# Value patches of a 5x5 correlation loaded in four transfers of 32 partitions, with the squares of pixels in another order

## The chip, the cores and the metric

The kernel runs on one core of a Trainium2 chip, as one launch. The metric is the device time of the launch in microseconds; three runs before the change gave 5152.57 (median), 5151.66 and 5160.39.

The core has five engines with a queue of instructions each: TensorE (PE: matmuls, and PEld, its weight loads), VectorE (DVE), ScalarE (ACT), GpSimd (POOL) and SyncE (SP). In this kernel SyncE issues every transfer; sixteen DMA engines carry them out. SBUF has 128 partitions; TensorE writes to PSUM, which DVE and ACT read.

## The reference

The input is x of shape (4, 512, 64, 64) in float32. Two layers follow each other. Layer 0 is linear attention with a second set of heads made by a depthwise 5x5 convolution:

```python
qkv = concat(h @ wq.T, h @ wk.T, h @ wv.T)          # 1536 channels
dw  = conv(qkv, dw_kernel 5x5, groups=1536)
pw  = conv(dw, pw_kernel 1x1, groups of 8)
f   = concat(qkv, pw) as heads of 24 channels: query 8, key 8, value 8
query, key = relu(...), relu(...)
scores = einsum("bhdn,bhen->bhde", [value, 1], key)   # sums over all 4096 pixels
out    = scores @ query, divided by its last row
y      = bn(proj_kernel @ out) + x
```

Layer 1 makes edge maps of y (Sobel, Laplace, diagonals), four 1x1 branches with GELU, a gate from their means, a 1x1 fusion, a norm over channels, GELU and a residual.

## The kernel before, in words

**Batches and groups.** There are four batches, each in four groups of 16 heads (128 channels per kind). A group works through keys, values and queries of its channels (`keys_and_values`, L544, and `queries`, L574, are lists of steps in a fixed order). The rest of layer 0 and all of layer 1 of a batch (`project_out`, `edge_branches`, `fuse_out`) are generators; `advance` (L868) calls them between the steps of the next batch's groups by planned costs, so that they fill TensorE. The order of TensorE's instructions is the one of the program; those of the other engines are put in order by a scheduler.

**Strips.** The 64x64 pixels of a batch go in eight strips of 512: each strip is every fourth row of one half of the image, eight rows of 64 pixels. `project` (L250) makes keys or queries of a strip and stores each in an SBUF tile `inp` in four transfers of 32 partitions (L266). `values` (L273) makes values with pixels on the partitions and writes them to a DRAM tensor `near` of blocks of four rows, 68 columns and 4 x 66 numbers per column (L291, four transfers a strip). Its borders are zeroed for the first two groups (L158: 34 rows, L160).

**The convolved heads.** Keys and queries are convolved directly on TensorE in 32x32 tiles (`convolve`, L382, 640 matmuls a half image). Values aren't: the scores of the convolved heads need the sum over pixels of convolved value times convolved key, so `correlate` (L432) multiplies convolved keys with the unconvolved values around each pixel, for all 5x5 shifts, and `weigh` (L454) takes the kernel's weights afterwards. The pixels are handled as squares of 4x4: in a contraction of 128, each partition stands for one square, 16 squares in a row of squares (x) by 8 rows of squares (b). A partition needs the values of its square and around it: 8 columns x 4 x 66 numbers of one block of rows in `near`, 8448 B in one run. That is a tile `near` of 128 x 2112 numbers, loaded by `load_near` (L420) in one transfer (L427), three buffers (`VALS`, L72), eight loads per group: two halves, two halves of the heads (jp), two blocks (b). Three are issued at the end of `keys_and_values`, then one each time two steps of `correlate` have used a tile up (L452).

**The order of squares.** The convolved keys come out of PSUM with the pixels in the order of the strip: row (8), x (16), n (4, the column in the square). ACT takes them out with ReLU, in the order column, x, row, and sums each partition's row by the way (`accum_out`, L402 to 405, `squares`, L109). Then `conv_turn` (L411) transposes 128 pixels at a time: one column n of all 128 squares, so that partition p holds square x = p // 8, row p % 8. The patch load uses the same order: its pattern in DRAM has 16 columns of squares, 8 rows of blocks and one run. `ksum` (L401) gathers the sums, two per bank (a half each), and `conv_sums` (L488) adds the halves.

What sets the order around the change: SyncE issues in its own order and stops at each transfer that has to wait. A patch load waits for the tile to be free (TensorE's last matmul on it) and for the stores into `near` (L291). The first matmul of `correlate` on a tile waits for its load.

Of the kernel before, what the change touches and what calls it, by code (L numbers as in the profile page):

```python
# [8 lines left out]
F32 = mybir.dt.float32  # L9
AF = mybir.ActivationFunctionType  # L10
ALU = mybir.AluOpType
AX = mybir.AxisListType

B, C, H, W = 4, 512, 64, 64
N = H * W
P = 128
# [11 lines left out]
BN1_SCALE = 1.0 / (1.0 + 1e-5) ** 0.5  # L28
SOBEL_EPS = 1e-8
LN_EPS = 1e-6  # L30

# [19 lines left out]
VROW = 4 * 66  # L53
# [21 lines left out]
def _span(d, n):  # L75

    return max(0, -d), n - max(0, d)
# [3 lines left out]
def conv_seq_kernel(  # L81
    ctx: ExitStack, tc, x, wqkv, dpk, wtab, proj, projc, pwk, bn0, consts, vec, watt1, batt1, watt2, wbr, wfuse, out
):
    nc = tc.nc
# [9 lines left out]
    mini = front.enter_context(tc.tile_pool(name="mini", bufs=2))  # L94
# [5 lines left out]
    def work_tile(name, n=512):  # L100
        return work.tile([P, 512], F32, tag="w", name=name)[:, :n]

    def ps_tile(name):
        return psum.tile([P, 512], F32, tag="ps", name=name)

    def quad_tiles(name):
        return [psum.tile([P, 512], F32, tag="quad", name=name) for _ in range(4)]

    def squares(ap):  # L109

        return ap.rearrange("p (b x n) -> p n x b", b=8, n=4)

    def rows(ap, width=W):
        return ap.rearrange("p (r c) -> p r c", c=width)
# [8 lines left out]
    def const_col(name, value):  # L123
        t = const.tile([P, 1], F32, name=name)
        nc.gpsimd.memset(t, value)
        return t
# [3 lines left out]
    grad_eps = const_col("grad_eps", 2 * SOBEL_EPS)  # L130
    ln_eps = const_col("ln_eps", LN_EPS)
    ones = const.tile([P, P], F32, name="ones")
# [82 lines left out]
    class Group:  # L215
# [166 lines left out]
        def convolve(self, t, half):  # L382
            banks = quad_tiles("cv")
            last = len(DXS) * 2 - 1
            for n, (dx, b) in enumerate((dx, b) for dx in DXS for b in range(2)):
                c0, c1 = _span(dx, W)
                for j in range(4):
                    for i in range(4):
                        q = slice(32 * i, 32 * i + 32)
                        nc.tensor.matmul(  # L390
                            rows(banks[i])[32 * j : 32 * j + 32, :, c0:c1],
                            lhsT=self.mat[t][q, j, (dx + 2) * 8 + 4 * b : (dx + 2) * 8 + 4 * b + 4, :],
                            rhs=inps[t][q, j, 8 * half + b : 8 * half + b + 8, c0 + dx : c1 + dx],
                            start=(n == 0), stop=(n == last),
                        )
            outs = []
            for i in range(4):
                o = work_tile("co")
                if t == KEY:
                    if half == 0 and i == 0:  # L400
                        self.ksum = mini.tile([P, 2, 4], F32, name="ksum")  # L401
                    nc.scalar.activation(  # L402
                        o.rearrange("p (n x b) -> p n x b", n=4, b=8), squares(banks[i]), AF.Relu,
                        accum_out=self.ksum[:, half, i : i + 1],
                    )
                else:
                    nc.scalar.activation(o, banks[i], AF.Relu)
                outs.append(o)
            self.conv[t] = outs
# [10 lines left out]
        def load_near(self, count):  # L420

            for _ in range(count):
                half, jp, b = at = next(self.nears, (None,) * 3)
                if half is not None:
                    self.near[at] = vals.tile([P, 8 * VROW], F32, name="near", tag="vals")
                    v = self.near_dram[jp, 8 * half + b]
                    nc.sync.dma_start(  # L427
                        out=self.near[at],
                        in_=bass.AP(v.tensor, v.offset, [[4 * VROW, 16], [(W + 4) * VROW, 8], [1, 8 * VROW]]),
                    )  # L430

        def correlate(self, half, jp, step):  # L432

# [54 lines left out]
        def conv_sums(self):  # L488

            total = mini.tile([P, 4], F32, name="ktotal")  # L490
            nc.vector.tensor_add(total, self.ksum[:, 0, :], self.ksum[:, 1, :])
            ps = ps_tile("ksum_ps")
            nc.tensor.matmul(ps[:, 0:4], lhsT=table["csum"], rhs=total, start=True, stop=True)
            self.kc = mini.tile([P, 4, 32], F32, name="kc_sb", bufs=1)
            for i in range(4):
                nc.vector.tensor_scalar(self.kc[:, i, :], hmask, ps[:, i : i + 1], None, ALU.mult)
# [531 lines left out]
```

## Time and profile before

| | |
|---|---|
| median of three runs | 5152.57 us |
| the profiled execution | 5156.95 us |
| its span (first to last instruction) | 5155.2 us |
| matmul clock granted, mean | 0.963 |
| HBM read, written | 622 MB, 214 MB |
| patch loads `near<-near` (L427) | 128 of 1056 KB, 138 MB; issue 556 ns median |
| matmuls of `correlate` (L442) | 8192, 330.7 us, 313 ns each |
| evictions of the convolved keys (L402) | 128 of 128x512, 597 ns each |

The page gives busy shares of each engine first, then the span in 40 slices, the DMA queue, the chain that ended last, and the costliest groups of instructions by line, operation and tiles. A name like `near<-near` is output and input; here the first is the tile in SBUF, the second the tensor in DRAM. Views of the trace list what each engine waited for and how long, the instructions in order of time, and the busy time, clock and DMA rate in a stretch that is asked for. The "DMA share" is the mean busy share of the sixteen DMA engines; it can pass 1 a little, where packets overlap.

### The profile page before, as it was taken

How to read it: one execution, taken by the hardware profiler on the slowest of the kernel's cores; microseconds unless marked ns; L12 is line 12 of the kernel's file. 1: busy time of each engine (PE TensorE's matmuls, PEld its weight loads, DVE VectorE, ACT ScalarE, POOL GpSimd, SP SyncE). 2: the span in 40 equal slices, each digit the busy share in tenths (PEclk: the TensorE clock that was granted, in tenths of full speed). 3: DMA queues.
4: the chain of work that ended last, by engine and by line, in shares of the span. 5: the costliest groups of instructions: out<-in, count | busy, mean ns of one | idle time of the engine just before them, and what ended most of it. 6: DMA issues, size and time to landing. Idle time of an engine off the chain costs nothing. (4 is left out here: it accounts for less than half of the span.)

```text
span 5155.2 us, 107053 instructions
## 1 busy us (share of the span) xinstructions
PE 4721.2 (92%) x46362; PEld 2727.4 (53%) x46362; DVE 2125.2 (41%) x2960; ACT 1622.7 (31%) x2585; POOL 384.0 (7%) x291
## 2 busy tenths in 40 slices
PE   7899999998999999799999998989989998899877
PEld 4556555454566655344466655444446565345443
DVE  1222221113655625211456543431135556246975
ACT  1111111001444524200235442430024445125765
POOL 0000000000000003200000000320000000000225
PEclk9999999999999999899999999999999999899989
DMA  6777777775666666767667666567666665674535
GB/s 184 187 193 195 185 212 191 179 160 140 194 184 193 194 191 188 212 153 150 168 178 208 170 191 186 180 202 172 154 177 173 178 183 160 176 179 117 153 103 169
DMA packets 645992, 910.30 MB, mean 177 GB/s; under 512 B 323688, under 2 KB 394376, under 8 KB 627088
## 3 DMA queue, kind: packets, MB, share of 16 engines
q1 hardware_dynamic: 645520, 903.45, 65.5%
q8 instruction: 364, 5.96, 0.5%
q14 instruction: 108, 0.88, 0.1%
HBM read 622.13 MB, written 213.98 MB: 162 GB/s over the span
## 5 line engine op out<-in xcount | busy, mean ns | idle before, releaser
L256 PE MATMUL proj<-xt,w_sb 128*128 128x512 f32 x2048 | 959.6, 611 | 58.3 <-DMA xt<-in_x 47.2
L642 PE MATMUL yps<-hd,fold_sb 128*128 128x512 f32 x2048 | 904.3, 598 | 25.2 <-DMA hd<-heads 23.1
L390 PE MATMUL cv<-inp,mat 32*32 32x512 f32 x20480 | 771.7, 621 | 121.2 <-issue 112.0
L256 PEld LDWEIGHTS proj<-xt,w_sb 128*128 128x128 f32 x2048 | 382.8, 195 | 534.8 <-issue 457.1
L642 PEld LDWEIGHTS yps<-hd,fold_sb 128*128 128x128 f32 x2048 | 385.8, 191 | 510.5 <-issue 474.2
L390 PEld LDWEIGHTS cv<-inp,mat 32*32 32x32 f32 x20480 | 422.1, 105 | 433.5 <-issue 270.8
L717 PE MATMUL br<-maps,wbr_sb 128*128 128x256 f32 x2048 | 491.6, 393 | 56.6 <-ACT maps L700 33.7
L278 PEld LDWEIGHTS val<-w_sb,xt 128*128 128x128 f32 x4096 | 471.5, 192 | 31.6 <-issue 21.9
L717 PEld LDWEIGHTS br<-maps,wbr_sb 128*128 128x128 f32 x2048 | 395.6, 196 | 173.5 <-issue 55.8
L278 PE MATMUL val<-w_sb,xt 128*128 128x128 f32 x4096 | 484.1, 276 | 0.1
L795 PE MATMUL zps<-ef,wf_sb 128*128 128x512 f32 x1024 | 462.6, 604 | 21.0 <-DVE z L799 7.2
L262 ACT COPY strip<-proj 128x512 f32<-128x512 f32 x256 | 149.3, 583 | 1017.1 <-PE proj L256 952.8
L647 DVE SCALAR_TENSOR_TENSOR yt<-yps,shift,xr 128x512 f32<-128x512 f32 x128 | 96.1, 751 | 905.1 <-PE yps L642 833.7
L442 PE MATMUL corr<-near,ckt 128*32 128x160 f32 x8192 | 330.7, 313 | 28.1 <-DMA near<-near 23.0
L236 POOL TENSOR_TENSOR mat<-dp_sb 128x1280 f32<-128x1280 f32 x32 | 77.3, 2416 | 3484.1 <-PE cv L390 2959.3
L795 PEld LDWEIGHTS zps<-ef,wf_sb 128*128 128x128 f32 x1024 | 194.2, 193 | 263.8 <-issue 227.8
L442 PEld LDWEIGHTS corr<-near,ckt 128*32 128x32 f32 x8192 | 252.4, 110 | 130.0 <-issue 58.2
L690 DVE TENSOR_TENSOR maps<-dv 128x1054 f32<-128x1054 f32 x128 | 162.6, 1270 | 304.1 <-PE br L717 304.1
L724 ACT ACTIVATE ef_o<-br,shift,scale 128x256 f32<-128x256 f32 x256 | 142.4, 560 | 314.9 <-PE br L717 314.4
L306 ACT ACTIVATE kt<-tr 128x512 f32<-128x512 f32 x128 | 76.1, 595 | 496.5 <-PE tr L304 488.9
L354 DVE RECIPROCAL rec<-rec 128x512 f32<-128x512 f32 x64 | 214.5, 3351 | 1.4
L402 ACT ACTIVATE co<-cv 128x512 f32<-128x512 f32 x128 | 74.6, 597 | 438.5 <-PE cv L390 438.4
(124 smaller groups left out, 4096.6 us busy)
## 6 DMA issues: line engine op xcount, KB each, us to landing
xt<-in_x SPq DMA_DIRECT2D x400, 512.0 KB
near<-near SPq DMA_DIRECT2D x128, 1056.0 KB
inp<-strip SPq DMA_DIRECT2D x1024, 64.0 KB
win<-y SPq DMA_DIRECT2D x128, 396.0 KB
near<-vt SPq DMA_DIRECT2D x512, 66.0 KB
y<-yt SPq DMA_DIRECT2D x128, 264.0 KB
yr<-y SPq DMA_DIRECT2D x128, 264.0 KB
xr<-in_x SPq DMA_DIRECT2D x128, 256.0 KB
```

Source lines behind the costliest of these rows:

```text
L256: nc.tensor.matmul(ps, lhsT=self.w[t][:, c, :], rhs=xs[self.b, j][c], start=(c == 0), stop=(c == NCH - 1))
L262: nc.scalar.copy(s, ps)
L278: nc.tensor.matmul(ps[:, ts(c, P)], lhsT=xs[self.b, j][n][:, ts(c, P)], rhs=self.w[VALUE][:, n, :], start=(n == 0), stop=(n == NCH - 1),)
L354: nc.vector.reciprocal(rec, rec)
L390: nc.tensor.matmul(rows(banks[i])[32 * j : 32 * j + 32, :, c0:c1], lhsT=self.mat[t][q, j, (dx + 2) * 8 + 4 * b : (dx + 2) * 8 + 4 * b + 4, :],
L442: nc.tensor.matmul(self.banks[jj][32 * i : 32 * i + 32, 160 * b : 160 * b + 160], lhsT=self.held["c", i][:, at : at + 32], rhs=v[:, 4 * n ...
L642: nc.tensor.matmul(ps, lhsT=fold_sb[g // NG][:, g % NG, ts(c, P)], rhs=hd[g], start=(g == 0), stop=(g == 2 * NG - 1),)
L647: nc.vector.scalar_tensor_tensor(yt[:, :, 1 : W + 1], rows(ps), shift0[:, c : c + 1], rows(xr), ALU.add, ALU.add)
L690: nc.vector.tensor_sub(flat[:, half : 3 * half - 2], dvs[:, 2 : 2 * half], dvs[:, 0 : 2 * half - 2])
L717: nc.tensor.matmul(rows(ps)[:, 4 * n : 4 * n + 4, :], lhsT=wbr_sb[:, k, c, :], rhs=rows(maps[c // 2][:, slot[k], c % 2, :], WB)[:, :, 0:W] ...
L724: nc.scalar.activation(o[:, n, :], ps[:, 256 * n : 256 * n + 256], AF.Gelu, bias=shift1[:, k : k + 1], scale=scale1[:, k : k + 1], accum_o ...
L795: nc.tensor.matmul(ps, lhsT=wf_sb[:, k, ts(c, P)], rhs=ef[k], start=(k == 0), stop=(k == 3))
```

## The change

A partition stands for another square. The 128 squares are cut in four quarters of 32: 8 columns of squares by 4 rows of squares. Partition p of the new order is quarter a, x half, then x (8), then row (4). So the patch load becomes four transfers, each to 32 partitions, with 8 columns of squares, 4 rows of blocks and the same run of 8448 B. The convolved keys have to come in the same order: each bank of 512 is taken out by two instructions of 256 pixels (four rows of the strip each) instead of one, with a sum each, so `ksum` has four sums per bank and `conv_sums` reduces them. Nothing else differs.

```diff
     def squares(ap):
-        return ap.rearrange("p (b x n) -> p n x b", b=8, n=4)
+        return ap.rearrange("p (b x n) -> p n x b", b=4, n=4)
...
                 if t == KEY:
                     if half == 0 and i == 0:
-                        self.ksum = mini.tile([P, 2, 4], F32, name="ksum")
-                    nc.scalar.activation(
-                        o.rearrange("p (n x b) -> p n x b", n=4, b=8), squares(banks[i]), AF.Relu,
-                        accum_out=self.ksum[:, half, i : i + 1],
-                    )
+                        self.ksum = mini.tile([P, 4, 4], F32, name="ksum")
+                    for a in range(2):
+                        nc.scalar.activation(
+                            o.rearrange("p (n a x b) -> p a n x b", n=4, a=2, b=4)[:, a],
+                            squares(banks[i][:, 256 * a : 256 * a + 256]), AF.Relu,
+                            accum_out=self.ksum[:, 2 * half + a, i : i + 1],
+                        )
...
                     self.near[at] = vals.tile([P, 8 * VROW], F32, name="near", tag="vals")
-                    v = self.near_dram[jp, 8 * half + b]
-                    nc.sync.dma_start(
-                        out=self.near[at],
-                        in_=bass.AP(v.tensor, v.offset, [[4 * VROW, 16], [(W + 4) * VROW, 8], [1, 8 * VROW]]),
-                    )
+                    for part in range(4):
+                        v = self.near_dram[jp, 8 * half + b + 4 * (part // 2), 32 * (part % 2)]
+                        nc.sync.dma_start(
+                            out=self.near[at][32 * part : 32 * part + 32, :],
+                            in_=bass.AP(v.tensor, v.offset, [[4 * VROW, 8], [(W + 4) * VROW, 4], [1, 8 * VROW]]),
+                        )
...
             total = mini.tile([P, 4], F32, name="ktotal")
-            nc.vector.tensor_add(total, self.ksum[:, 0, :], self.ksum[:, 1, :])
+            nc.vector.tensor_reduce(total, self.ksum.rearrange("p a i -> p i a"), AX.X, ALU.add)
```

## The prediction

> **What bounds the kernel now.** I read the page first, then the waits of TensorE, then the waits of SyncE's queue, then the timeline around one correlation, and last the busy time and DMA rate of a few short stretches. Busy shares first:
>
> ```profile
> PE 4721.2 (92%) x46362; PEld 2727.4 (53%) x46362; DVE 2125.2 (41%) x2960; ACT 1622.7 (31%) x2585; POOL 384.0 (7%) x291
> ...
> q1 hardware_dynamic: 645520, 903.45, 65.5%
> ```
>
> TensorE is the bound (4721 of 5155 us). The order of its instructions is the same before and after, with the same shapes, so the change can only move the 434 us in which it stands idle. What ends those, from the waits view (total us, times, longest):
>
> ```profile
> PE cv L390 <- issue: 112.0, 46, 4.4
> PE proj L256 <- DMA xt<-in_x: 47.2, 14, 12.1
> ...
> PE yps L642 <- DMA hd<-heads: 23.1, 6, 9.8
> PE corr L442 <- DMA near<-near: 23.0, 7, 19.6
> ...
> PE mix L484 <- DMA projc<-in_projc: 14.2, 4, 4.9
> ...
> PE proj L256 <- ACT ckt L417: 9.2, 5, 2.9
> ```
>
> The patch loads themselves cost TensorE 23.0 us, 19.6 of them in one wait; the other six are 0.3 to 0.9 us each. So a patch load comes just in time, seldom late. The timeline shows why: TensorE frees a patch tile at 148.3, SyncE issues the load at 149.29 (0.56 us), and its patches are needed after two thirds of the 192 matmuls that start at 153.32, near 158.3.
>
> ```profile
> 145.78 2.55 PE L442 MATMUL corr<-near,ckt 128*32 128x160 f32 x64
> ...
> 153.32 7.51 PE L442 MATMUL corr<-near,ckt 128*32 128x160 f32 x192
> ```
>
> Now the rate of a patch load. Four stretches (window, its length, five engines, clock, DMA share, GB/s): 2147 to 2151 is the load of two fold tables, 128 rows on both sides; 2156 to 2159 lies, by the order of issue, in the four hd loads from cheads; 160 to 164 is patch loads alone; 10 to 13 holds the two zero borders of 34 rows issued at 8.57.
>
> ```profile
> 2147.00:2151.00 4.00, 0.00 (x0) 0.00 (x0) 0.00 (x0) 0.00 (x0) 0.00 (x0) 0.73 1.00 418
> 2156.00:2159.00 3.00, 0.00 (x0) 0.00 (x0) 0.00 (x0) 0.00 (x0) 0.00 (x0) 0.50 1.13 272
> 160.00:164.00 4.00, 4.00 (x105) 2.36 (x104) 2.18 (x4) 0.00 (x0) 0.00 (x0) 1.00 1.00 218
> 10.00:13.00 3.00, 3.00 (x24) 2.53 (x22) 1.85 (x3) 2.20 (x4) 2.03 (x1) 1.00 0.15 57
> ```
>
> With all sixteen engines busy (share 1.00) the fold load moves 418 GB/s, 26.1 per engine, and the patch load only 218, 13.6 per engine. The cheads load has the patch load's form (16 by 8 rows in DRAM into 128 partitions) and is slow too. [...] The last line shows a second thing: a transfer of 34 rows keeps about 0.15 x 16 = 2.4 engines busy, so the outer counts decide how many engines take part.
>
> **The change, part by part.**
>
> 1. *The patch loads (128 of 1056 KB).* One transfer with outer counts 16 (DRAM) and 128 (partitions) becomes four with 8 and 32. Bytes and runs of 8448 B stay. Today: 1.081 MB / 218 GB/s = 4.96 us. The unknown is how many engines take part and at what rate, so four prices: sixteen at 26.1 GB/s, 2.59 us (-2.37); unchanged, 4.96; eight at 26.1, 209 GB/s, 5.17 us (+0.21); eight at 13.6, 9.92 us (+4.96). [...] So the step trades a full pace on half of the engines for a half pace on all, and lands 0.2 us later. [...] On the path: the 7 waits for patches and the 3.9 us wait for xt at 118, which follows three patch loads: 8 x 0.21 = **+1.7 us**. If the pace were the slow one, see the second rival.
>
> [...]
>
> 2. *Issues on SyncE.* Each load is four issues. Rows: this load's own issue has a median of 556 ns, the 32-partition strip store (L266) 586 ns, the 34-row border (L158) 268 ns. So 4 x 0.586 - 0.556 = +1.79 us a load at most, 4 x 0.268 - 0.556 = +0.52 at least; I take 1.79, the row with 32 partitions, 229 us over 128 loads. Queued behind are whatever SyncE issues next: strip stores, xt, w_sb, heads. Its cover is the time in which SyncE waits for compute:
>
> ```profile
> SPq L651 <- DVE yt L647: 440.8, 103, 17.2
> SPq L729 <- ACT ef_o L724: 320.9, 91, 23.3
> SPq L234 <- POOL mat L236: 317.5, 28, 20.6
> ```
>
> With the next six rows of that view, all on compute, it is 2156 us. After the burst of three loads at 156.5 SyncE issues xt and then stands until 183 for the dp table; there 5.4 us more are hidden. A part moves in 5.17 / 4 = 1.3 us and is issued in 0.59, so within a load the issue is faster than the move. I cost it at **0**; uncovered it is 1.79 us per late transfer (third rival). SyncE's transfers carry eight semaphores in turn, and an issue waits for the transfer eight before it; four parts use four of the eight. The fifth transfer behind a load now waits for its first part, where the eighth waited for the whole: the first part lands early, so I cost that at 0 too. The first part alone waits for the tile; the other three wait for no compute that the first hasn't waited for.
>
> 3. *ACT.* 128 evictions of 128x512 (L402, 597 ns, and 206 for the accumulator) become 256 of 256 columns. In the timeline of ACT at 114 they start 0.59 us apart, four in 2.36 us. Size of a half: copies of 512 and 128 columns take 583 and 263 ns, so 256 is an estimated 370, started 0.37 us apart with its accumulator (the 512 starts 0.59 apart at 0.597); eight are 3.0 us, +0.64. Upper end: the 128x256 Gelu with accumulator (L724) starts 0.55 apart, eight are 4.4 us, +2.0. The new access pattern has a dimension more; L402 reads PSUM in strides today and costs what the plain L407 costs (597 and 600 ns), so strides add nothing. 32 convolutions, 20 us of ACT, which is 31% busy. On the path where TensorE waits for ACT right after the eviction: ctr for co (2 waits), ctr for rq (2), proj for co (1): 5 x 0.64 = **+3.2 us**, 10 at the upper end. The five waits for ckt don't take it: in the one at 2632, ACT stood idle for 1.6 us and 1.7 us between co and ckt. Two more table loads (1.28 us each) appear in ACT's order, off the path: 0.
>
> 4. *DVE.* The sum of ksum is a reduction of 16 values instead of an add of 4 (402 ns, 16 times). DVE is 41% busy: 0, at most some 0.1 us x 16.
>
> 5. *Order.* DVE, ACT and SyncE move little: of SyncE's other 3555 instructions 2836 keep their place and the mean shift is under one. The border rows of y and three dp and pw loads leave a place at 116 to 126 us; some parts go between the win loads at 1208. I cost it at 0, with 10 us to either side: half of the 20.4 us wait of heads_ps there.
>
> **Sum.** The profiled execution took 5156.95 us (span 5155.2, 1.75 around it). +1.7 +3.2 gives 5161.9. The median of the three runs, 5152.57, lies 4.4 below that execution, so I forecast 5157.5, rounded to **5158**.
>
> **Rivals.**
>
> - *Faster: sixteen engines, or a freed half that helps.* The parts run at the fold load's pace (2.59 us a load). The six short waits go (3.5 us), the long one shrinks by 2.4, and 128 x 2.37 = 303 us of DMA time come free, 9% of its busy share; the 84.5 us for xt, hd and projc shrink by as much, 7.6. Together -13.5 + 3.2 = -10: 5142. At most all 23.0 and the 3.9 go: 5129. For: 218 against 418. Against: the 34-row line. Chance 0.18.
> - *Slower: eight engines, still slow.* If the 13.6 GB/s is not a matter of which engines write where, a load takes 9.92 us. It is needed about 10 us after its tile is freed (148.3 to 158.3), so the fourth load of each of the 16 groups is late by the whole 4.96: +79 us, 5237. It decides once a load takes clearly longer than today's 4.96. Against: the fold load moves rows of 8 KB at 26.1 GB/s per engine, so long rows are not slow in themselves. Chance 0.07.
> - *Slower: SyncE.* The cover is missing where TensorE waits for a transfer already: xt 14, patches 7, hd 6, projc 4, 31 waits. Each 1.79 later is 55 us; half of them 28. With the forecast's 4.9: 5185. It decides where SyncE goes from a patch load to the awaited transfer without a wait for compute. For: bursts of three loads at the ends of groups. Chance 0.27.
> - *It does not do what it says*: sixteen engines with two partitions each and the old pace; the time is the forecast's. In its 0.48.
>
> **How the numbers follow.** Forecast 0.48, faster rival 0.18, SyncE 0.27, slow engines 0.07. The forecast's own range is 5148 to 5168 (order, upper ACT end). For 8 in 10, I leave out the slow engines and the outer parts of the other rivals: 5135 to 5190. A measurement of this kernel tells about 0.2%, 10 us, from no change: faster means under 5142, slower over 5163. Faster gets 0.13 of its rival and 0.06 of order: 0.19; slower the SyncE and slow-engine cases but 0.03, and 0.08 of the forecast: 0.39; the rest, 0.42, is within.
>
> **What would show it.** Right: in a stretch of patch loads the DMA share falls to about 0.5 with GB/s still near 210; the queue's share falls from 65.5% to near 60%; corr's wait for near stays between 20 and 30 us; the part's issue has a median near 0.59; L402 shows 256 evictions near 370 ns. Wrong: a patch stretch at 400 GB/s (first rival), at 110 (second), or TensorE's waits for xt and hd up by 20 us or more (third).

## The result

The changed kernel is slower: 5192.05 us median of five runs (5178.43 to 5196.08), against 5158.97 for the kernel before on the same chip (five runs, 5151.66 to 5160.39). The ratio is 1.0063, interval 1.0046 to 1.0081: 33 us. The forecast was 5158 and the range ended at 5190. The profiled execution took 5184.32 us, its span 5182.5, 27.3 longer than that of before.

The page of the changed kernel, busy shares and queue:

```profile
PE 4718.6 (91%) x46362; PEld 2737.6 (53%) x46362; DVE 2126.5 (41%) x2960; ACT 1643.6 (32%) x2843; POOL 383.1 (7%) x291
...
q1 hardware_dynamic: 647568, 903.46, 60.0%
...
L404 ACT ACTIVATE co<-cv 128x256 f32<-128x256 f32 x256 | 93.9, 397 | 364.0 <-PE cv L391 353.9
```

What TensorE waited for (us, times, longest):

```profile
PE proj L257 <- DMA xt<-in_x: 102.7, 21, 11.4
PE cv L391 <- issue: 42.0, 29, 3.5
...
PE mix L488 <- DMA projc<-in_projc: 33.6, 4, 9.0
PE yps L646 <- DMA hd<-heads: 25.6, 7, 10.0
PE corr L446 <- DMA near<-near: 24.9, 6, 20.6
...
PE zps L799 <- DMA ef<-ef: 20.2, 2, 15.1
PE hid_ps L774 <- DMA watt_sb<-in_watt: 17.4, 2, 12.5
```

The names: xt is the input of a strip for `project`, projc a group's weights for `mix`, hd the heads read back, ef and watt_sb belong to layer 1. Two things moved, in opposite directions. The waits for awaited transfers rose: xt from 47.2 to 102.7, projc from 14.2 to 33.6, ef from 2.6 to 20.2, the attention weights from 8.1 to 17.4. The stalls inside the convolution, which the view calls `issue`, fell from 112.0 to 42.0. The wait for the patches themselves hardly changed (23.0 to 24.9).

A stretch of patch loads (window, length, five engines, clock, DMA share, GB/s):

```profile
156.00:160.00 4.00, 4.00 (x105) 2.46 (x104) 2.18 (x4) 0.00 (x0) 0.00 (x0) 1.00 0.52 209
```

Share 0.52 at 209 GB/s, as forecast: half of the engines at twice the pace. In the trace a packet of 8448 B takes 319 ns (median) where it took 619.

**Where the loss is.** SyncE's instructions around the second group's `mix`, first before, then after (start, duration, instruction):

```profile
425.25 0.55 SPq L427 DMA_DIRECT2D near<-near  x1
425.85 0.58 SPq L624 DMA_DIRECT2D hd<-heads  x1
426.48 0.42 SPq L476 DMA_DIRECT2D projc<-in_projc  x1
```

```profile
442.01 7.39 SPq L431 DMA_DIRECT2D near<-near  x10
449.44 0.47 SPq L480 DMA_DIRECT2D projc<-in_projc  x1
```

TensorE's answer, before and after:

```profile
435.63 1.10 PE L484 MATMUL mix<-projc,pwb 128*128 128x512 f32 x2 [1.91 <-DMA projc<-in_projc]
```

```profile
459.11 2.05 PE L488 MATMUL mix<-projc,pwb 128*128 128x512 f32 x2 [8.14 <-DMA projc<-in_projc]
```

Before, one patch load of 0.55 us stood ahead of projc. After, ten parts and 7.39 us do: each load is four issues, and the scheduler has also put two and a half loads there and not one. The same at the end of a group: three loads before xt took 5.12 us of SyncE at 347.56, twelve parts take 10.50 at 355.37, and xt is issued at 366.48 and not at 352.73.

The scheduler moved xt as well. In the second and the third group two of the four xt that stood ahead of a strip's stores into `near` stand behind them in the changed kernel; before and after, with TensorE's wait:

```profile
399.45 2.44 SPq L266 DMA_DIRECT2D inp<-strip  x4
401.94 1.08 SPq L247 DMA_DIRECT2D xt<-in_x  x2
405.74 3.02 SPq L291 DMA_DIRECT2D near<-vt  x4
```

```profile
410.53 2.47 SPq L267 DMA_DIRECT2D inp<-strip  x4
416.82 3.70 SPq L292 DMA_DIRECT2D near<-vt  x4
420.57 2.36 SPq L248 DMA_DIRECT2D xt<-in_x  x4
```

```profile
425.97 3.09 PE L257 MATMUL proj<-xt,w_sb 128*128 128x512 f32 x4 [4.54 <-DMA xt<-in_x]
```

TensorE waits 86.3 us for xt up to 900 us, where it waited 31.6. Four waits in the middle of a group are 26.5 us of that; they end 5 to 8 us after the issue of the xt, so it is the issue that is late there. Four at the ends of groups are 27.5 us, and there the data are late: xt lands 12 to 14 us after its issue. At the wait that ends at 379.4, the 384 packets of three xt come in two halves, the second from 375.4 to 381.3, as the last patch packets run out (377.5); before, they came in one stretch, 363.5 to 370.2, and were there when TensorE came to its matmul. That fits half of each xt standing behind the parts, on the engines that the parts use, though the traces name no engine.

By 900 us SyncE had spent 94.9 us on patch loads, against 21.1. Batch 0 (to about 860 us) has no second layer beside it, so a late transfer there soon is a wait of TensorE. The stretch to 900 us, before and after:

```profile
0.00:900.00 900.00, 816.01 (x11236) 497.12 (x11236) 194.98 (x301) 144.64 (x297) 31.00 (x33) 0.97 0.71 193
```

```profile
0.00:900.00 900.00, 768.47 (x10594) 472.31 (x10596) 186.41 (x289) 138.92 (x338) 28.59 (x32) 0.94 0.59 182
```

TensorE did 642 matmuls fewer in the same 900 us, and its granted clock fell from 0.97 to 0.94. Since its order of instructions is the same in both, I can subtract the start of each matmul before from that after ("drift" from here on): +58.5 us at 900, +27.0 at the end. All of the loss falls in batch 0, and half of it is won back later.

**Where the gain is.** TensorE around the second convolution of the first group's keys, before and after:

```profile
160.77 4.08 PE L390 MATMUL cv<-inp,mat 32*32 32x512 f32 x89
168.36 5.87 PE L390 MATMUL cv<-inp,mat 32*32 32x496 f32 x128 [3.51 <-issue]
177.02 3.97 PE L390 MATMUL cv<-inp,mat 32*32 32x504 f32 x103 [2.79 <-issue]
```

```profile
156.86 4.04 PE L391 MATMUL cv<-inp,mat 32*32 32x512 f32 x87
161.08 4.38 PE L391 MATMUL cv<-inp,mat 32*32 32x496 f32 x128 [0.17 <-issue]
165.63 4.19 PE L391 MATMUL cv<-inp,mat 32*32 32x504 f32 x105 [0.17 <-issue]
```

A stall stands after 128 matmuls, that is 256 instructions with their weight loads; 46362 pairs in 364 packets of the page's "instruction" queue q8 (16 KB each) are 127 pairs a packet. So at such a point the next packet of TensorE's instructions would be needed (an inference from these counts). In the trace of before, the stalls over 0.8 us in the convolutions (42, together 115.8 us) end 1.45 us after a packet of q8 has landed (median; a tenth of them below 1.27 and a tenth above 1.58). During the 3 us before that packet began, patch packets kept 0.72 of the engines busy (median). After the change 21 such stalls are left, 43.9 us, and the median of that share is 0. Counting all transfers, the engines were full in those 3 us (median 1.02 before, 1.00 after); before the other q8 packets that landed in a convolution, the medians were 0.83 and 0.61. So it is full engines that go with a stall, and the patch loads filled them most often. From first to last matmul the 64 convolutions took 892.9 us before and 786.4 after.

Of these 106.5 us 71.5 are less idle time before the matmuls (121.2 to 49.7) and 34.9 less busy time in them (771.7 to 736.8). The second part goes with the clock. After the stall of 3.51 us in before, the granted clock is about a half, and the 128 matmuls take 5.87 us; without the stall they take 4.38. Two stretches, before and after:

```profile
169.00:172.00 3.00, 3.00 (x75) 1.85 (x64) 0.00 (x0) 0.00 (x0) 0.00 (x0) 0.52 1.00 214
```

```profile
161.00:165.00 4.00, 3.92 (x128) 2.33 (x128) 0.00 (x0) 0.00 (x0) 0.00 (x0) 1.00 0.76 249
```

Weighing the time of the convolutions' matmuls by the clock that wasn't granted gives 46.8 us before and 12.2 after, a difference of 34.6.

So the 27.3 us are -106.5 in the convolutions and +133.8 elsewhere: xt +55.5, projc +19.4, ef +17.6, attention weights +9.3, slower `proj` matmuls (959.6 to 975.9 us busy; the same weighing gives 24.5 and 39.6 us lost to the clock) +16.3, the rest many small ones.

### The profile page after: what moved, and what is told of

It is laid out like the page before. It is cut to its first block, busy times and chain, and to the rows that moved or that the text cites. A ratio compares the mean times of both kernels' runs of the same rounds, so it can differ in the third digit from the quotient of the medians.

```text
span 5182.5 us, 107736 instructions
## 1 busy us (share of the span) xinstructions
PE 4718.6 (91%) x46362; PEld 2737.6 (53%) x46362; DVE 2126.5 (41%) x2960; ACT 1643.6 (32%) x2843; POOL 383.1 (7%) x291
## 5 line engine op out<-in xcount | busy, mean ns | idle before, releaser
L257 PE MATMUL proj<-xt,w_sb 128*128 128x512 f32 x2048 | 975.9, 620 | 112.0 <-DMA xt<-in_x 102.7
L391 PE MATMUL cv<-inp,mat 32*32 32x512 f32 (+1 forms) x20480 | 736.8, 597 | 49.7 <-issue 42.0
L799 PE MATMUL zps<-ef,wf_sb 128*128 128x512 f32 x1024 | 468.8, 610 | 37.6 <-DMA ef<-ef 20.2
L279 PEld LDWEIGHTS val<-w_sb,xt 128*128 128x128 f32 x4096 | 474.0, 193 | 31.5 <-issue 21.7
L446 PE MATMUL corr<-near,ckt 128*32 128x160 f32 x8192 | 332.9, 315 | 31.4 <-DMA near<-near 24.9
L404 ACT ACTIVATE co<-cv 128x256 f32<-128x256 f32 x256 | 93.9, 397 | 364.0 <-PE cv L391 353.9
```

The source lines that it names most:

```text
L257: nc.tensor.matmul(ps, lhsT=self.w[t][:, c, :], rhs=xs[self.b, j][c], start=(c == 0), stop=(c == NCH - 1))
L279: nc.tensor.matmul(ps[:, ts(c, P)], lhsT=xs[self.b, j][n][:, ts(c, P)], rhs=self.w[VALUE][:, n, :], start=(n == 0), stop=(n == NCH - 1),)
L391: nc.tensor.matmul(rows(banks[i])[32 * j : 32 * j + 32, :, c0:c1], lhsT=self.mat[t][q, j, (dx + 2) * 8 + 4 * b : (dx + 2) * 8 + 4 * b + 4, :],
L446: nc.tensor.matmul(self.banks[jj][32 * i : 32 * i + 32, 160 * b : 160 * b + 160], lhsT=self.held["c", i][:, at : at + 32], rhs=v[:, 4 * n ...
L799: nc.tensor.matmul(ps, lhsT=wf_sb[:, k, ts(c, P)], rhs=ef[k], start=(k == 0), stop=(k == 3))
```

## The experiments

Theory: four issues on SyncE (their time, and what they stand ahead of) cost more than the 33 us, and the half of the DMA engines that comes free gives a part back in the convolutions. Rivals: the evictions in halves; the new order of squares; parts that land late, and hold up the data of transfers behind them. The table takes the ratio from the timed runs against before on the same chip; the other columns are of the profiled executions: the 64 convolutions from first to last matmul, TensorE's wait for xt and projc together, and the drift against the profile of before at 900 us and at the end (one execution each, on several chips: good for ten us, not for less).

```
                                 ratio (interval)         convolve  xt+projc  drift 900  end
changed kernel                   1.0063 (1.0046-1.0081)     786       136       +58      +27
e1  halves alone                 1.0017 (1.0001-1.0032)     896        60        -7       +3
e2  three small transfers more   1.0078 (1.0060-1.0097)     897        88       +34      +36
e3  two transfers of 64          1.0069 (1.0048-1.0089)     879        95       +32      +16
e6  four parts, not in batch 0   0.9917 (0.9899-0.9934)     812        62        -2      -47
e4  four parts from GpSimd       0.9858 (0.9838-0.9879)     856        53       -15      -81
e4b one transfer from GpSimd     0.9964 (0.9950-0.9978)     891        60        +6      -22
e5  two transfers of 8x8         1.0314 (1.0287-1.0340)     820       167      +110     +156
e8  changed, xt from GpSimd      0.9893 (0.9877-0.9910)     793        12       -39      -75
e8b before, xt from GpSimd       1.0014 (1.0001-1.0027)     903        11       -18      -15
e9b batch 0 parts from ScalarE   0.9961 (0.9949-0.9973)     780        69       +12      -34
e10 e6 with xt from GpSimd       0.9952 (0.9934-0.9969)     819         -       -23      -60
e11 mixed                        0.9871 (0.9848-0.9895)     840        36       -28      -93
```

(Before: 893 and 61. In e10 the view of waits shows neither.)

**e1, the evictions alone.** One transfer and the old order; only ScalarE's part of the change.

```diff
-        return ap.rearrange("p (b x n) -> p n x b", b=8, n=4)
+        return ap.rearrange("p (b x n) -> p n x b", b=4, n=4)
...
-                    nc.scalar.activation(
-                        o.rearrange("p (n x b) -> p n x b", n=4, b=8), squares(banks[i]), AF.Relu,
-                        accum_out=self.ksum[:, half, i : i + 1],
-                    )
+                    for a in range(2):
+                        nc.scalar.activation(
+                            o.rearrange("p (n x a b) -> p a n x b", n=4, a=2, b=4)[:, a],
+                            squares(banks[i][:, 256 * a : 256 * a + 256]), AF.Relu,
+                            accum_out=self.ksum[:, 2 * half + a, i : i + 1],
+                        )
```

> The kernel before, with only the change on ScalarE: evictions of the convolved keys in two halves and four sums a bank, in the old order of squares; the patch load stays one transfer. Theory SyncE (the +33 us come from four issues in place of one, in the first batch, less a gain in the convolutions): 0 to +10 us against before; TensorE's waits for xt stay near 47 us and its stalls inside the convolution (cv behind issue) near 112 us. Rival ScalarE/order: the loss is in the halves and in what the scheduler moved, so +25 us or more here.

Measured 1.0017 (5159.48 against 5155.26 us, +4; by the ratio +9). Stalls 112.4, xt 45.6, as before. The halves are about a quarter of the loss; the upper end of the interval, 1.0032, would be half of it.

**e2, the issues alone.** The load as before, and behind it three transfers of 32 partitions by 64 B.

```diff
+                    for part in range(1, 4):
+                        v = self.near_dram[jp, 8 * half + b + 4 * (part // 2), 32 * (part % 2)]
+                        extra = mini.tile([P, 16], F32, name="extra", tag="extra", bufs=12)
+                        nc.sync.dma_start(
+                            out=extra[32 * part : 32 * part + 32, :],
+                            in_=bass.AP(v.tensor, v.offset, [[4 * VROW, 8], [(W + 4) * VROW, 4], [1, 16]]),
+                        )
```

> The kernel before (one transfer, old order) with three more transfers behind each patch load, of 32 partitions by 64 B into a scratch tile that nobody reads: SyncE's extra issues without the new form of the load. Theory SyncE: the loss of the first batch comes back without the gain: +35 to +60 us, if these issues take 0.5 to 0.65 us each (less in proportion if they are shorter), waits for xt up by 25 us or more, stalls inside the convolution still near 112 us. Rival DMA (the new form lands late, on half of the engines): within 10 us of before, waits for xt near 47 us.

Measured 1.0078, +40 us. The issues of the small transfers and TensorE's waits (in the first line: minimum, median and maximum in ns):

```profile
L434 SPq DMA_DIRECT2D extra<-near x384: 644/645/2762, 95.2 to 4307.9; - x192
```

```profile
PE cv L390 <- issue: 115.4, 51, 4.6
...
PE mix L491 <- DMA projc<-in_projc: 35.9, 4, 11.9
```

The three issues alone, with no bytes to speak of, cost as much as the whole change does net of its gain; the stalls are untouched. The expectation had the extra wait at xt, which rose by 4.6 only; it is at projc (+21.7), before which twelve of the small issues stand. So it matters which transfer the issues happen to stand ahead of. In this kernel xt keeps its place before the strip's stores, and no parts move on half of the engines: issue time by itself gives the wait for projc, not the one for xt.

**e3, two transfers of 64 partitions.** Order of squares and evictions as changed.

```diff
-                    for part in range(4):
-                        v = self.near_dram[jp, 8 * half + b + 4 * (part // 2), 32 * (part % 2)]
+                    for part in range(2):
+                        v = self.near_dram[jp, 8 * half + b + 4 * part]
                         nc.sync.dma_start(
-                            out=self.near[at][32 * part : 32 * part + 32, :],
-                            in_=bass.AP(v.tensor, v.offset, [[4 * VROW, 8], [(W + 4) * VROW, 4], [1, 8 * VROW]]),
+                            out=self.near[at][64 * part : 64 * part + 64, :],
+                            in_=bass.AP(v.tensor, v.offset, [[4 * VROW, 16], [(W + 4) * VROW, 4], [1, 8 * VROW]]),
                         )
```

> The changed kernel with the same new order of squares, but the patch load in two transfers of 64 partitions (16 columns by 4 rows) and not in four of 32 (8 by 4). Theory SyncE with the gain from free DMA engines: one extra issue a load and not three, so +12 to +25 us of loss; all sixteen engines are taken again at the slow pace (share near 1.0 in a stretch of patch loads, packets near 613 ns), so the stalls inside the convolution are back near 112 us and the gain is gone: +10 to +25 us against before. Rival order (the new order of squares itself costs or gains): as the changed kernel, +33, and stalls near 42 us.

The gain went as expected, a stretch of loads and the stalls:

```profile
160.00:164.00 4.00, 2.48 (x82) 0.94 (x78) 0.00 (x0) 0.00 (x0) 0.00 (x0) 1.00 0.96 211
```


```profile
PE cv L391 <- issue: 107.2, 45, 4.8
PE proj L257 <- DMA xt<-in_x: 56.0, 15, 11.2
PE mix L488 <- DMA projc<-in_projc: 38.6, 4, 13.0
```

All engines are taken again (0.96 at 211 GB/s, packets 584 ns), and the stalls are back at 107. So it is the form of the transfers that took them away, not the order of squares. The size of the loss was a miss: +33 us measured, 25 at most expected. SyncE's extra time on patch loads to 900 us is only 24.8 (45.9 against 21.1), the drift +31.9. The rest is place: in this kernel too two and a half loads (five halves) stand ahead of projc, where one stood before, and the second and third group's xt behind the stores (waits of 4.8 and 3.5 us).

**e6, one transfer in batch 0, four later.** The form and the order of squares are chosen by the batch; evictions in halves throughout.

```diff
+                    if self.b == 0:
+                        v = self.near_dram[jp, 8 * half + b]
+                        nc.sync.dma_start(
+                            out=self.near[at],
+                            in_=bass.AP(v.tensor, v.offset, [[4 * VROW, 16], [(W + 4) * VROW, 8], [1, 8 * VROW]]),
+                        )
+                    else:
+                        for part in range(4):
...
```

> One transfer and the old order of squares in batch 0, four transfers and the new order in batches 1 to 3; evictions in halves throughout. Theory SyncE with the gain: batch 0 has nothing beside it that hides SyncE and loses nothing now (drift of TensorE near 0 at 900 us in place of +58), the later batches keep their gain in the convolutions (-30 us): 20 to 35 us faster than before. Rival catching up (the later batches only win back what batch 0 made late, through slack in the order): within 10 us of before.

Measured 0.9917: 42 us faster than before (5113.21 against 5155.26), more than expected. Drift -1.5 at 900 us and -46.9 at the end; xt and projc wait 62 us, as in before. The later batches take the gain (convolutions after batch 0: 682 to 598 us) and, with their second layer beside them, SyncE's issues cost less than that. So the catching-up rival falls: with nothing lost in batch 0 there is the gain all the same.

**e9b, another issuer in batch 0.** The changed kernel; the same four transfers, issued in batch 0 by ScalarE.

```diff
-                        nc.sync.dma_start(
+                        (nc.scalar if self.b == 0 else nc.sync).dma_start(
```

> The changed kernel with the parts of batch 0 issued by ScalarE, those of batches 1 to 3 by SyncE as in the change: the same form of transfer, another issuer, in the batch that lost. Theory SyncE: TensorE's drift against before at 900 us falls from +58 to between -25 and +15 (ScalarE is busy 16% of that batch; its parts may hold its evictions up for some us); later batches as in the change, -20 to -30; 5110 to 5160. Rival DMA or order of squares (batch 0 loses by the form, whoever issues it): drift at 900 stays over 40 and the time near 5192.

Measured 0.9961 (5119.73 against 5139.23), drift +12.3 at 900 us in place of +58.5. The edit changes nothing but the queue of 128 parts, so some 46 of the 58 us come from their standing in SyncE's queue and not from the form by itself. The parts' data are in a DMA queue of their own then (q10 on the page), so this run does not tell late issues from data held up behind the parts. The wait for patches rose to 50.3 us (28.4 of them in batch 0); ScalarE's own order, in which parts and evictions take turns, would explain it, but no run shows that.

**e8 and e8b, the awaited transfers away from SyncE.** In the changed kernel and in before, xt, projc and pw are issued by GpSimd; the patch loads stay on SyncE.

```diff
-                nc.sync.dma_start(out=xt, in_=x[self.b, j, :, 2 * n : 2 * n + 2, :])
+                nc.gpsimd.dma_start(out=xt, in_=x[self.b, j, :, 2 * n : 2 * n + 2, :])
...
-            nc.sync.dma_start(out=rest, in_=projc[self.g])
+            nc.gpsimd.dma_start(out=rest, in_=projc[self.g])
...
-            nc.sync.dma_start(out=pw, in_=pwk[self.g])
+            nc.gpsimd.dma_start(out=pw, in_=pwk[self.g])
```

> The changed kernel, its four parts still issued by SyncE, but the transfers that TensorE waited for most, xt, projc and pw, issued by GpSimd, so that they no longer stand behind the parts in SyncE's order. Theory SyncE: the waits for xt and projc fall from 136 us to under 75; the patch loads keep their form and their eight engines, so the 64 convolutions stay near 786 us (stalls near 42); the time is 5095 to 5145. Rival DMA (xt is late because the engines that carry it are behind the parts, not because it is issued late): waits for xt and projc stay over 110 and the time over 5165.

> Control: the kernel before with xt, projc and pw issued by GpSimd. Theory SyncE: there was less of a queue on SyncE to get past, so it gains less than the changed kernel does from the same move: 0 to 35 us faster than before, the convolutions stay near 893 us. If it gains as much as the changed kernel does (60 us or more), the move is worth that by itself and says nothing on the four issues.

Measured 0.9893 with the change and 1.0014 without, where a gain of 0 to 35 us was expected. The changed kernel's waits:

```profile
PE corr L446 <- DMA near<-near: 53.0, 12, 25.3
PE cv L391 <- issue: 46.6, 37, 2.9
...
PE proj L257 <- DMA xt<-in_x: 11.8, 1, 11.8
```

This is the cleanest test of the queue. Where xt does not stand behind the patch loads, the change is worth 1.2% (0.9893 to 1.0014); where it does, it costs 0.6%. The same move gained before nothing, and the changed kernel 1.7%, some 87 us of its 5192. The rival of parts that land late expected xt over 110: the one wait left is 11.8 us. That refutes it as it was put, but xt has also left the parts' DMA queue (q0 on the page, not q1), so issues, places and data held up in the queue all go at once here. The trace of the changed kernel separates them (above): late issues at projc and in the middle of groups, late data at their ends. What has grown is the wait for the patches (53.0).

**e4 and e4b, the patch loads from GpSimd.** In e4 the four parts of the change, in e4b the one transfer of before; all else as there.

```diff
-                        nc.sync.dma_start(
+                        nc.gpsimd.dma_start(
```

> The changed kernel with the four parts issued by GpSimd and not by SyncE; all else as changed. Theory SyncE with the gain: SyncE gets back the 70 us of issues of the first batch, the convolutions keep their gain (64 of them take 786 us from first to last matmul, against 893 before), so the time falls below before, to some 5080 to 5115 us, if GpSimd's own issues and its waits for free tiles delay nothing; TensorE's waits for xt and projc fall back to 62 us or less from 136. Rival DMA (parts land late, whoever issues them): still over 5165, with waits for xt near 100 us.

> Control for the run with GpSimd: the kernel before, with its one transfer a load issued by GpSimd. Theory SyncE with the gain: takes away only 0.56 us a load from SyncE (71 us in all, 18 in the first batch), convolutions stay slow near 893 us: between 15 us faster and 5 us slower than before. If it is as fast as the four parts from GpSimd, the gain there is the other queue and not the form of the load.

Measured 0.9858 (5078.24 against 5162.19, -84 us) and 0.9964 (-21 us, a little more than the 15 expected). e4's loss in batch 0 is gone (drift -15.3). But the reason I gave for its gain was half wrong. A stretch of its loads, and its stalls:

```profile
168.00:172.00 4.00, 2.34 (x77) 0.93 (x49) 0.00 (x0) 0.00 (x0) 1.60 (x3) 1.00 1.04 300
```

```profile
PE cv L391 <- issue: 94.3, 50, 3.5
```

The same four transfers run on all engines here (1.04 at 300 GB/s, where SyncE's ran at 0.52 and 209), so loads are quicker, and most of the stalls are back: 856 us in the convolutions, not 786. "The gain stays" failed; e4 gains by SyncE's relief and by faster loads. The traces don't tell which engine carried which part, and no run shows why the issuer makes this difference.

**e5, 64 partitions on half of the engines.** Before, with the load in two transfers of 8 columns by 8 rows.

```diff
-                    v = self.near_dram[jp, 8 * half + b]
+                    for part in range(2):
+                        v = self.near_dram[jp, 8 * half + b, 32 * part]
...
-                            in_=bass.AP(v.tensor, v.offset, [[4 * VROW, 16], [(W + 4) * VROW, 8], [1, 8 * VROW]]),
+                            out=self.near[at][64 * part : 64 * part + 64, :],
+                            in_=bass.AP(v.tensor, v.offset, [[4 * VROW, 8], [(W + 4) * VROW, 8], [1, 8 * VROW]]),
```

> [...]

Measured 1.0314 (5321.94 us, two runs), where 5225 or more was expected if the slow engines' rival came true, and 5140 to 5180 if not: the slow engines' case, and twice as dear as the +79 us of that rival. Packets stay at 615 ns (median); a stretch and the waits:

```profile
172.00:176.00 4.00, 3.96 (x66) 3.10 (x68) 0.36 (x1) 0.00 (x0) 0.00 (x0) 0.65 0.51 122
```

```profile
PE proj L256 <- DMA xt<-in_x: 141.1, 26, 19.9
PE corr L443 <- DMA near<-near: 66.2, 13, 24.0
```

The share is 0.51 as in the changed kernel, but 122 GB/s and not 209, 15.0 GB/s an engine and not 25.1. So eight engines alone don't make a patch packet fast. Nor do four partitions an engine, on average, as the changed kernel has them: e3 has 64 partitions on all sixteen engines (share 0.96 at 211 GB/s, 13.7 an engine), and its packets take 584 ns. Of these forms only 32 partitions on eight engines (share 0.52) are fast (319 ns). Why, no run shows; the runs show the rate. For the gain the run is of use too: its packets are as slow as before, but half of the engines stay free, and the stalls are 62.9 us and not 112.0.

**e10, e6 with xt from GpSimd.** The two edits together.

> The kernel with one transfer in batch 0 and four parts later (5113 us, 42 below its before), and xt, projc and pw on GpSimd besides. Theory SyncE with the gain: both effects add up where the later batches still wait behind SyncE (xt 43 us, projc 20 us there): 5070 to 5110. If the later batches have enough cover on SyncE, within 10 us of 5113 less what the control with xt on GpSimd alone gains.

Measured 0.9952, not faster than e6 alone (0.9917). The waits that remain are for patches (42.1), the stalls (70.4) and, at the start, 11.1 us for the first weights. The two effects don't add up: the later batches seem to have cover enough on SyncE, as the second reading had it.

**e11, SyncE relieved differently in each batch.** Batch 0: xt, projc and pw from GpSimd, parts from SyncE. Later: parts from GpSimd.

```diff
-                nc.sync.dma_start(out=xt, in_=x[self.b, j, :, 2 * n : 2 * n + 2, :])
+                (nc.sync if self.b else nc.gpsimd).dma_start(out=xt, in_=x[self.b, j, :, 2 * n : 2 * n + 2, :])
...
-                        nc.sync.dma_start(
+                        (nc.gpsimd if self.b else nc.sync).dma_start(
```

(projc and pw as in e8.)

> The changed kernel with SyncE relieved in each batch of what the runs so far showed best: in batch 0 GpSimd issues xt, projc and pw and SyncE the four parts (that run stood 39 us ahead of before at 900 us); in batches 1 to 3 GpSimd issues the four parts and SyncE xt (that run gained 66 us after 900 us). Theory SyncE: the two add up to about 100 us less than before, ratio 0.978 to 0.984. If the batches are not apart (what is won in the first is waited for later), no better than the run with all parts on GpSimd, 0.986.

Measured 0.9871 (5077.92 against 5150.79), the same as e4 within the intervals; 0.978 to 0.984 was expected. In the profiled execution batch 0 ended 28 us ahead and not 39. Why the gains don't add up stays open. e4, with the simpler edit, is the best version run: 84 us faster than before.

## Why the prediction was wrong

- **Step 1, the patch loads, right in pace and size.** No row of before shows its term, eight engines at 26.1 GB/s and so +0.21 us a load; the changed kernel then ran so (share 0.52 at 209 GB/s, 8448 B in 319 ns, which is 26.5 GB/s), with the wait for patches 24.9 against a forecast of 20 to 30 and the queue's share 60.0%. In the stretches read, the share of busy engines went with the outer counts as long as SyncE issued: 0.15 for 34 rows, 0.52 for 8 by 4, 0.51 for 8 by 8, 0.96 for 16 by 4, 1.00 for 16 by 8. From GpSimd the 8 by 4 parts ran at 1.04 (e4), so the counts alone don't decide it. e5 shows the slow engines' rival to be real for another shape, and dearer than its +79: about 160 us, since xt is late too.
- **Step 1 missed the gain.** The half of the engines that lies free was worth nothing in the forecast, and in the faster rival only what xt, hd and projc would gain by it. What gained was TensorE: its `issue` stalls in the convolution, 112.0 us and the longest line of my own list of waits, were copied and never asked about. They are 42.0 now and the convolutions 106 us shorter, a third of it by the clock that the stalls cost. That the form of the load does this is shown by e3 (same order and bytes, engines full, stalls 107) and e6. That it is the fetch of TensorE's instructions is shown only by place and by the full engines before it: the stalls end some 1.4 us after such a packet. An xt behind the patches was priced at 0.21 us of waiting: the four waits for xt at the ends of groups in batch 0 are 27.5 us.
- **Step 2 failed: "I cost it at 0".** The size per load was near: four issues at 652 ns, +2.05 us and not +1.79. The cover was read from a total, 2156 us of SyncE's waits for compute over the whole kernel. Batch 0 has cover in total as well (SyncE waited some 363 us for compute to 900 us before, 300 after), but none between the parts and projc, and no second layer beside it. There 32 loads bring 66 us of issues, and 58 us are lost. With the load unchanged, e2's three issues alone cost 34 us to 900. The semaphores, put at 0 too, weren't free: to 900 us SyncE stood 52.6 us until a patch load or a part had landed, 26.9 before. The forecast's third rival (SyncE, 5185, chance 0.27) was the right mechanism in the main: it named the ends of groups, xt and projc, and its mark, 20 us more wait for xt, came true with 55. Its sum was right by cancellation: e8 against the changed kernel puts the part of SyncE's queue (issues, places and data) at some 87 us, and the gain it lacked takes most of it back.
- **Step 5, order, failed in two places.** "Mean shift is under one" was true and hid the shifts that counted: ten parts ahead of projc where one load had stood, and xt behind a strip's stores (4.5 us of waiting each in the second and third group). e2 and e3 pay for the first (35.9 and 38.6 us at projc), e3 for the second.
- **Step 3, ScalarE, right as far as the runs tell.** e1 gives +4 to +9 us for +3.2 with an upper end of 10 (its interval reaches 16); a half takes 397 ns for an estimated 370.
- **Faster rival, wrong in its reason.** A freed half does help, but by another road than xt, hd and projc.

## What to carry to other kernels

Cover for a queue's issues has to be read where the issues fall: a total over a kernel whose stages differ says little, and the question for each added issue is what stands right behind it and who waits for that. And the order in which a scheduler puts a queue has to be read at the awaited transfers, not as a mean. Stalls of the bounding engine that no semaphore explains are a term of the sum too; look at what the DMA engines do in the same microseconds. A load that keeps half of the engines at full pace can serve better than one that keeps them all at half pace, if the transfers that are waited for go by another queue than it does (e8, 0.9893, and e9b in one batch, 0.9961), or where other work covers its issues (e6, 0.9917). e4, the fastest, put the load on another queue and by that on all engines again (1.04).

## What the runs showed of the hardware that was not expected

- TensorE stalled in its convolutions when transfers filled the DMA engines: 42 stalls of 0.8 us or more before the change, 2.8 us each on average, and a median busy share of 1.02 over the 3 us ahead of the instruction packet that landed 1.45 us (median) before a stall's end. Of the 41 distances from one such stall to the next 39 are whole multiples of 127.4 matmuls, to a tenth; by the page's counts an instruction packet has 127 of them with their weight loads. Most likely TensorE waits for its instructions; no run shows the fetch itself.
- An issue on SyncE costs by its pattern, not by its bytes: 645 ns for 32 partitions of 64 B, 652 ns for 32 partitions of 8448 B, 584 for 64 partitions as 16 by 4, and 556 for 128 (medians); two of 64 as 8 by 8 took 1.32 us together (e5).
- How many partitions there are does not set the rate alone: 64 as 16 by 4 on all engines (e3) moved 211 GB/s, beside 209 for the parts of 32, and 64 as 8 by 8 on half of the engines (e5, share 0.51) moved 122.
- A stall costs more than its length: after the one of 3.51 us the granted clock was 0.52 from 169 to 172 us, and over the first 900 us it was 0.97 before and 0.94 after, with 74 us more of waiting for xt and projc.
